# An audio tower on one core: a planner that counts overlapping neighbours, exponentials taken from the score banks, and later joins

## The chip, the cores and the metric

The kernel runs on one core of a Trainium2 chip. The metric is the device time of one execution in microseconds. Times below are the median of three runs, with their lowest and highest, or come from one profiled execution and its trace. Engines are named as in the profile: PE (TensorE matmul), PEld (its weight loads), DVE (VectorE), ACT (ScalarE), POOL (GpSimd), SP (the queue that issues DMAs).

## The reference

For each of 32 audio clips of 160000 samples:

```python
h = frames(x) @ DCT.T                          # 313 frames of 512 samples -> 512 features
a = layernorm(h)
Q, K, V = xpos(a @ W_Q), xpos(a @ W_K, downscale), a @ W_V       # 8 heads of 64
p = softmax(Q @ K.T) * Dmat                    # Dmat: per-head decay with distance
h = h + (silu(a @ W_G) * groupnorm(p @ V)) @ W_O
a = layernorm(h)
theta = a[..., None, :] / (1 + |W|) + B_param  # 256 units x 512 features, per frame
i = round(theta * 4096 / 2pi) mod 4096
s = sum(sin_table[i] * attn_sin, -1); c = sum(cos_table[i] * attn_cos, -1)
h = h + silu(c @ proj_cos.T + s @ proj_sin.T)
```

The costly part is the last layer: a sine and a cosine for each of 32 x 313 frames, 256 units and 512 features.

## The kernel before, in words

**Sines.** The 256 units are cut into 8 blocks of 32 (`UNITS`). A round (`ffn_round`, L746) treats one block for the sequences that are then in the ring, at most 8; a sequence joins at round `STARTS[q]`, stays 8 rounds (one for each block) and leaves. A round's work is cut into slots of 24 rows of 313 values (16 when the ring has one sequence). For each slot DVE computes integer indices from features and frequencies (L800, one operation for each unit, feature chunk and run of sequences, so a short ring means many short operations), adds a quarter turn (L816) and masks both copies (L823); ACT takes the sine of each copy (L837, two instructions of 12 x 2 x 313 = 7512 values); PE sums over features into four PSUM banks (L860). There are five index buffers and five sine buffers, and a slot needs two of each.

**Attention.** The front of the network (`attention`, L362) is done for one sequence at a time in one set of buffers and in the other four PSUM banks, and has to be finished before that sequence joins. Its stages: transform, layernorm, transpose, values (`rows` into `x.v`), then two halves of (two rotations, two sets of scores), exponentials, eight heads (transpose, decay, product), gate, group norm, output projection. A set of scores (L432) is, three times: a pair of matmuls into two banks, a maximum over each row on DVE (L448), and a subtraction that writes the scores minus the maximum to `x.prob` (L452). Later ACT takes exponentials in place from `x.prob`: two instructions of 3756 columns (L469) and sums on DVE (L484), or, in the *ACT mode*, 24 instructions of 313 columns which also sum (L473). The ACT mode, in which ACT also makes the copies out of PSUM, is chosen where the ring has at most `NARROW` sequences when the attention begins. Before the exponentials ACT loads their table, and after them it returns to the table with the sine (L477). Sequence 0 has an opening of its own (`opening`, L962); sequence 1 follows it at once.

**Order.** Nothing is scheduled by hand and nothing by the framework: `Plan` (L56) collects operations with a key (its due place), an engine, a duration in ns, and what they read and write. `emit` (L99) simulates the engines with these durations and issues the instructions in the order that comes out; on each engine the ready operation with the lowest key goes first. Results cross to another engine after 300 ns (`WAIT`), or 800 (`SLACK`) for the attentions. Each engine runs its instructions in that order. `lend` (L80): when ACT stands idle in the plan and DVE has more ready operations than the one it takes, ACT takes one of those for which a second version is given; index operations have one (L806).

**Due places.** A key counts slots of one sine: a sequence in a round is 2 x 32 x 4 / 24 = 10.67 keys. The attentions' starts are spread so that each is done `LEAD` keys before its sequence joins; the loop at L1297 takes the smallest spacing that some later sequence asks for, and each attention's steps get keys spread over its spacing (`SHARE`, L30).

Of the kernel before, what the change touches and what calls it, by code (L numbers as in the profile page):

```python
# [21 lines left out]
P = 128  # L22
# [33 lines left out]
class Plan:  # L56
# [13 lines left out]
    def add(self, key, eng, dur, fn, r=(), w=(), other=None):  # L70
# [9 lines left out]
    def lend(self, t, e, at, free, ready, coming):  # L80

        if ready["ACT"] or free["ACT"] > t or (coming["ACT"] and coming["ACT"][0][0] <= t):
            return None
        while coming["DVE"] and coming["DVE"][0][0] <= t:
            _, i = heapq.heappop(coming["DVE"])
            heapq.heappush(ready["DVE"], (self.ops[i][0], i))
        held = sorted(ready["DVE"])[int(free["DVE"] <= t):]
        for o in sorted((o for o in held if o[1] in self.other),
                        key=lambda o: (self.other[o[1]][0] > self.ops[o[1]][2], o)):
            if True:  # L90
                start = max(free["ACT"], at[o[1]])
                if coming["ACT"] and coming["ACT"][0][0] < start + self.OWN * self.other[o[1]][0]:
                    continue
                ready["DVE"].remove(o)
                heapq.heapify(ready["DVE"])
                return o[1], start
        return None

    def emit(self):  # L99
# [31 lines left out]
        left = len(ops)  # L131
        while left:
            best = None
            for e in free:
                if ready[e]:
                    t = free[e]
                elif coming[e]:
                    t = max(free[e], coming[e][0][0])
                else:
                    continue  # L140
                if best is None or t < best[0]:
                    best = (t, e)
            t, e = best
            lent = self.lend(t, e, at, free, ready, coming)
            if lent:
                i, t = lent
                e = "ACT"
                dur, fn = self.other[i]
            else:
# [15 lines left out]
        return max(free.values())  # L165
# [3 lines left out]
def tile_audio_tower(ctx: ExitStack, tc: tile.TileContext, t: dict, out: bass.AP):  # L169
# [192 lines left out]
    def attention(plan, keys, sq, x, eng, swap_m=None, early=False, quick=False):  # L362
# [13 lines left out]
        def residual(key, load):  # L376
            for i in range(NT):
# [20 lines left out]
        rows(plan, step("rows"), x, x.xnT, wv_d, (x.k("xnT"),), range(NT - 1, -1, -1),  # L398
             ("wv_d",))
        copy(plan, step("copy"), eng, NT * HOP, x.v[:N], W3.rearrange("n j (g d) -> n j g d", d=P),  # L400
             x.banks(0, 1, 2), hs)
        plan.add(step(), "POOL", 4000, lambda: nc.gpsimd.memset(x.v[0:1, : NT - 1], 0.0), (), hs)  # L402
# [4 lines left out]
        def rotary(g):  # L407
            key = step("rotary")
            y = x.sets[g % len(x.sets)]
            qk, kq = x.qk[g % 2], x.k("u", g % 2)  # L410
# [6 lines left out]
            else:  # L417
                copy(plan, key, eng, 2 * S, x.raw, y.W[:, 0:2, :S], y.banks(0, 1), probs[-1:])
                for i in range(2):
# [10 lines left out]
                     probs[-2:], (kq,))  # L430
# [27 lines left out]
        for half in range(2):  # L458
            for g in (2 * half, 2 * half + 1):
                rotary(g)  # L460
            for g in (2 * half, 2 * half + 1):
                scores(g)


        key = step("exps")
        for a0 in (0, H // 2):
            def exps(a0=a0):
                if eng == "DVE":
                    nc.scalar.activation(x.prob[:N, a0 : a0 + H // 2], x.prob[:N, a0 : a0 + H // 2],  # L469
                                         AF.Exp)  # L470
                for a in range(a0, a0 + H // 2):
                    for i in range(NT if eng == "ACT" else 0):
                        nc.scalar.activation(x.prob[:N, a, i, :], x.prob[:N, a, i, :], AF.Exp,  # L473
                                             accum_out=x.sm[:N, i, a : a + 1])
                if a0:

                    nc.scalar.activation(x.lu[:1, 0:1], x.lu[:1, 0:1], AF.Silu)  # L477
            plan.add(-1e9 if a0 else key, "ACT", 1400 + (7700 if eng == "ACT" else 3350), exps,
                     probs[a0 : a0 + H // 2] if early else probs if not a0 else (),
                     [*probs[a0 : a0 + H // 2], x.k("sm", a0), x.k("lu")])  # L480
        if eng == "DVE":
# [264 lines left out]
    def ffn_round(plan, k0, blk, ring, final):  # L746
# [25 lines left out]
        for parts in slots:  # L772
# [53 lines left out]
            for k in (1, 0):  # L826
# [11 lines left out]
                plan.add(key, "ACT", 115 + 0.8333 * E, sines, every(x[1 - k]),  # L838
# [617 lines left out]
```

## Time and profile before

| | |
|---|---|
| median of 3 runs | 18152.65 us (18149.81 to 18154.47) |
| the profiled execution | 18155.45 us |
| its span, first to last instruction | 18153.7 us |
| ACT busy | 17989.7 us, 99% |
| DVE busy | 17132.7 us, 94% |
| PE busy | 14314.5 us, 79% |
| granted TensorE clock | 0.935 |

Busy time is the union of an engine's instructions. A group line of the profile gives line, engine and operation, tiles and shapes, count, then busy us and mean ns of one, then the idle us just before them and what ended most of that. Neighbouring instructions of one engine can overlap by some 0.1 us, so a mean duration is longer than the distance between two starts. The answers by stretch give, for each stretch of the span, its length, the busy us of each engine (or of one line's instructions) with the count, the granted clock and the DMA share and rate.

### The profile page before, as it was taken

Reading aid. Unit: us, or ns where it says so; the run is one execution under the profiler, and the core shown is the slowest. Engines: PE = TensorE matmul, PEld = TensorE weight load, DVE = VectorE, ACT = ScalarE, POOL = GpSimd, SP = SyncE. Lnnn points to the kernel's source line nnn. Section 1 sums busy time; section 2 is a strip of 40 time slices with the busy share of each in tenths; the row PEclk is TensorE's granted clock in tenths of the full one; section 3 lists DMA queues with packets and bytes.
Section 4 is the critical chain, followed back from the end, with each engine's and each line's share of the span. In section 5 each row is a group of like instructions: output and inputs, shape, how many; then the busy total and the mean of one; then the engine's idle time right before and its main releaser. Section 6 shows DMA issues by size and latency. Waiting matters only on the chain.

```text
span 18153.7 us, 322090 instructions
## 1 busy us (share of the span) xinstructions
PE 14314.5 (79%) x146495; PEld 6447.3 (36%) x146495; DVE 17132.7 (94%) x12295; ACT 17989.7 (99%) x3448; POOL 126.5 (1%) x40
## 2 busy tenths in 40 slices
PE   8888888887778777878777787777777777766667
PEld 4434433433333333333333333333333333322222
DVE  8999999999999999999999999999999999888888
ACT  7999999999999999999999999999999999999999
POOL 0000000000000000000000000000000000000000
PEclk9999999999999999999999999999999999989889
DMA  3222211111111111111111111111111111100011
GB/s 115 74 63 64 67 56 57 53 51 47 45 52 53 53 52 41 53 54 51 51 50 47 53 53 53 52 41 53 54 51 50 48 48 54 46 28 27 28 33 58
DMA packets 603597, 943.16 MB, mean 52 GB/s; under 512 B 121290, under 2 KB 344138, under 8 KB 589430
## 3 DMA queue, kind: packets, MB, share of 16 engines
q1 hardware_dynamic: 602230, 922.56, 16.4%
q8 instruction: 1148, 18.81, 0.4%
q14 instruction: 219, 1.79, 0.0%
HBM read 818.35 MB, written 103.94 MB: 51 GB/s over the span
## 4 chain that ended last, share of the span: by engine, by line
ACT 40%; PE 18%; DVE 8%; issue 7%; DMA 0%; ACTq 0%; SPq 0%; DVEq 0%
ACT trig L837 40%; PE PS L860 15%; DVE ix L800 3%; DVE ix L823 2%; PE PS L341 2%; DVE ix L816 1%; PE PS L357 1%; ACT a_prob L469 0%; DMA a_u<-in_frames 0%; DVE part L882 0%; PE PS L561 0%; ACT L477 0%; DVE a_h L267 0%; PE PS L523 0%; ACTq L837 0%
## 5 line engine op out<-in xcount | busy, mean ns | idle before, releaser
L837 ACT ACTIVATE trig<-ix 128x7512 f32<-128x7512 int16 (+2 forms) x2780 | 17384.1, 6346 | 50.1 <-PE PS L860 30.6
L860 PE MATMUL PS<-trig,hot 128*32 128x313 f32 x131072 | 10449.9, 463 | 3662.4 <-ACT trig L837 3594.1
L860 PEld LDWEIGHTS PS<-trig,hot 128*32 128x32 f32 x131072 | 4391.7, 117 | 9590.2 <-ACT trig L837 4876.7
L800 DVE TENSOR_SCALAR ix<-xT,f 128x2504 int16<-128x2504 f32 (+7 forms) x5329 | 6418.7, 1264 | 90.4 <-ACT trig L837 67.1
L823 DVE TENSOR_SCALAR ix<-ix 128x7512 int16<-128x7512 int16 (+3 forms) x1668 | 5583.9, 3362 | 42.5
L816 DVE TENSOR_SCALAR ix<-ix 128x7512 int16<-128x7512 int16 (+2 forms) x1390 | 2908.8, 2093 | 553.3 <-ACT trig L837 450.7
L357 PE MATMUL PS<-a_xnT,a_ring 128*128 128x313 f32 x4960 | 1468.1, 439 | 8.9 <-DVE a_prob L425 6.9
L341 PE MATMUL PS<-a_ring,a_u 128*105 128x512 f32 x2232 | 1067.4, 611 | 53.6 <-DMA a_u<-in_frames 19.6
L357 PEld LDWEIGHTS PS<-a_xnT,a_ring 128*128 128x128 f32 x4960 | 893.4, 189 | 588.4 <-issue 276.5
L341 PEld LDWEIGHTS PS<-a_ring,a_u 128*105 128x105 f32 x2232 | 349.9, 171 | 629.3 <-issue 585.3
L341 PE MATMUL PS<-a_ring,a_xnT 128*105 128x512 f32 x744 | 353.9, 608 | 3.5 <-DVE a_xnT L267 1.8
L500 PE MATMUL PS<-ident,a_prob 105*105 105x105 f32 x2232 | 288.8, 272 | 70.5 <-DVE a_prob L512 47.1
L448 DVE TENSOR_REDUCE a_mx<-PS 105x2 f32<-105x626 f32 x372 | 298.6, 803 | 29.0 <-PE PS L443 28.9
L512 DVE TENSOR_TENSOR a_prob<-PS,a_u 105x939 f32<-105x939 f32 x248 | 280.3, 1130 | 38.4 <-PE PS L500 34.3
L500 PEld LDWEIGHTS PS<-ident,a_prob 105*105 105x105 f32 x2232 | 236.5, 176 | 223.7 <-issue 140.6
L452 DVE TENSOR_TENSOR a_prob<-PS,a_mx 105x626 f32<-105x626 f32 x372 | 301.3, 810 | 12.8
L443 PE MATMUL PS<-a_u 64*105 64x313 f32 x1488 | 258.9, 453 | 8.5 <-DVE a_prob L452 7.0
L523 PE MATMUL PS<-a_prob,a_h 105*64 105x313 f32 x1488 | 240.9, 443 | 6.6 <-DVE a_prob L512 6.5
L484 DVE TENSOR_REDUCE a_sm<-a_prob 105x6 f32<-105x1878 f32 x112 | 228.8, 2103 | 8.6 <-ACT a_prob L469 8.6
L402 POOL MEMSET a_h<- 1x1024 f32 x31 | 124.0, 4002 | 15023.3 <-DVE a_h L267 14393.9
L806 ACT ACTIVATE ix<-xT,f 128x313 int16<-128x313 f32 (+6 forms) x206 | 195.3, 1008 | 0.2
L425 DVE TENSOR_TENSOR a_prob<-PS,a_prob 128x1252 f32<-128x1252 f32 x124 | 180.7, 1457 | 10.5 <-PE PS L357 9.8
(157 smaller groups left out, 2606.0 us busy)
## 6 DMA issues: line engine op xcount, KB each, us to landing
hot<-in_hot SPq DMA_DIRECT2D x1344, 128.0 KB
xT<-xT_d SPq DMA_DIRECT2D x88, 1252.0 KB
a_u<-in_decay SPq DMA_DIRECT2D x248, 260.5 KB
a_ring<-in_proj SPq DMA_DIRECT2D x128, 256.0 KB
a_ring<-in_dct SPq DMA_DIRECT2D x124, 256.0 KB
a_ring<-wv_d SPq DMA_DIRECT2D x124, 256.0 KB
a_ring<-in_wq SPq DMA_DIRECT2D x124, 256.0 KB
a_ring<-in_wk SPq DMA_DIRECT2D x124, 256.0 KB
```

The source lines that it names most:

```text
L341: lambda c=c, i=i, k=k, to=to: nc.tensor.matmul(x.W[:N, to, :], lhsT[:, c, ROW0[i] : ROW0[i] + N], x.ring[k], start=(c == 0), stop=(c == N ...
L357: lambda c=c: nc.tensor.matmul(y.W[:, bank, :S], w[:, c, :], x.xnT[:, c, :], start=(c == 0), stop=(c == NC4 - 1)),
L443: nc.tensor.matmul(y.W[:N, b + a, :S], qk[a * DH : a * DH + DH, 0, ROW0[i] : ROW0[i] + N], qk[a * DH : a * DH + DH, 1, :], start=True, sto ...
L448: lambda b=b, m=m, y=y: nc.vector.tensor_reduce(m[:N], y.W[:N, b : b + 2, :S], AX.X, ALU.max),
L452: lambda i=i, b=b, m=m, y=y: nc.vector.tensor_tensor(x.prob[:N, 2 * g : 2 * g + 2, i, :], y.W[:N, b : b + 2, :S], m[:N].unsqueeze(2).to_br ...
L500: nc.tensor.transpose(y.W[:N, jj, ROW0[i] : ROW0[i] + N], x.prob[:N, a, i, ROW0[j] : ROW0[j] + N], ident[:N, :N],)
L512: nc.vector.tensor_tensor(x.prob[:N, a], y.W[:N, :NT, :S], w3, ALU.mult)
L800: nc.vector.tensor_scalar(ix[:, x[0], at * S : (at + nb) * S], xT[:, y, b0 * S : (b0 + nb) * S], f[:, 0, n : n + 1], f[:, 1, n : n + 1], A ...
L816: nc.vector.tensor_scalar(ix[:, x[1], :E], ix[:, x[0], :E], float(LUT // 4), None, ALU.add)
L823: nc.vector.tensor_scalar(ix[:, i, :E], ix[:, i, :E], LUT - 1, LUT // 2, ALU.bitwise_and, ALU.bitwise_xor)
L837: nc.scalar.activation(o, i, AF.Sin, bias=-PI32, scale=ANG)
L860: nc.tensor.matmul(sums_W[:, p, :][g * 32 : g * 32 + 32, :S], now["hot", hot[n // 4 * 4, c]][:, n % 4, k, :], trig[:, z, at * S : (at + 1) ...
```

## The change

The planner gets two constants: `OVER`, by which an engine is free again before an operation's end (85 ns on DVE, 100 on ACT, half the duration at most), and `AFTER`, 35 ns, which an operation waits for the result of one before it on its own engine. The duration of a sine grows from 115 to 197 ns plus 0.8333 ns a value. An operation may belong to a group; once ACT has begun one, ACT and DVE are *held*: in the plan, ACT issues only that group's operations, and DVE only these or operations of at most 900 ns, and nothing is lent, until ACT has done the last.

Sequences 1 to 7 (`burst`) do all four rotations first, with two of the query and key pairs kept in the buffer `x.h`, and then one group of 24 steps: a matmul into one bank, a maximum (negated) on DVE, and an exponential on ACT that reads that bank with the maximum as its bias, writes `x.prob` and sums. The subtraction, and the sums on DVE, are gone for them. The values, which use `x.h`, move behind the group. The starts, the lead, and the choice of the ACT mode change with it.

```diff
-STARTS = (0, 2, 4, *range(6, 35))
+STARTS = (0, 3, 5, 7, *range(10, 38))
-FROM, TO, LEAD, NARROW = -900.0, -899.0, 8.0, 2
+FROM, TO, LEAD, NARROW, BURSTS = -900.0, -899.0, 6.0, 1, 8
...
+    OVER = {"DVE": 85.0, "ACT": 100.0}
+    AFTER = 35.0
...
-        if ready["ACT"] or free["ACT"] > t or (coming["ACT"] and coming["ACT"][0][0] <= t):
+        if self.held or ready["ACT"] or free["ACT"] > t or (coming["ACT"] and coming["ACT"][0][0] <= t):
...
+    def next_held(self, e, at, free, ready, coming):
+
+        some = [(max(free[e], at[i]), self.ops[i][0], i) for _, i in (*ready[e], *coming[e])
+                if self.group.get(i) == self.held or (e == "DVE" and self.ops[i][2] <= self.SHORT)]
+        if not some:
+            return None
+        t = min(some)[0]
+        _, i = min((k, i) for s, k, i in some if s <= t)
+        return t, e, i
+
+    SHORT = 900.0
...
+                if self.held and e in ("ACT", "DVE"):
+                    t = self.next_held(e, at, free, ready, coming)
...
             fn()
+            if i in self.group and e == "ACT":
+                todo[self.group[i]] -= 1
+                self.held = self.group[i] if todo[self.group[i]] else None
             free[e] = t + dur
+            free[e] -= min(self.OVER.get(e, 0.0), dur / 2)
...
-                at[j] = max(at[j], end + (0.0 if same else self.wait[i]))
+                at[j] = max(at[j], end + (self.AFTER if same else self.wait[i]))
...
+        if not burst:
+            values()
+        if burst:
+            mine = x.h.rearrange("p i d -> p (i d)")[:, : NC4 * S].rearrange("p (g i s) -> p g i s", g=2, s=S)
+            qks, kqs = [*x.qk, mine[:, 0], mine[:, 1]], [*us, hs[0], hs[1]]
+        else:
+            qks, kqs = [*x.qk, *x.qk], [*us, *us]
...
+        def together():
+
+            gid = ("exps", sq)
+            n_all = 2 * NC4 * NT
+            for z in range(n_all):
+                g, i, a, b = z // 2 // NT, z // 2 % NT, z % 2, z % 4
+                qk = qks[g][a * DH : a * DH + DH]
+                m, km = x.mx[b // 2][:N, a : a + 1], x.k("mx", b)
+
+                def exps(hd=2 * g + a, i=i, b=b, m=m, z=z):
+                    nc.scalar.activation(x.prob[:N, hd, i, :], x.W[:N, b, :S], AF.Exp, bias=m, scale=1.0,
+                                         accum_out=x.sm[:N, i, hd : hd + 1])
+                    if z == n_all - 1:
+                        nc.scalar.activation(x.lu[:1, 0:1], x.lu[:1, 0:1], AF.Silu)
+                plan.slack = plan.WAIT
+                plan.add(-1e9 + z, "PE", 350, lambda i=i, b=b, qk=qk: nc.tensor.matmul(
+                    x.W[:N, b, :S], qk[:, 0, ROW0[i] : ROW0[i] + N], qk[:, 1, :], start=True, stop=True),
+                    (kqs[g], kqs[-1]), x.banks(b), group=gid)
+                plan.add(-1e9 + z, "DVE", 490, lambda b=b, m=m: nc.vector.tensor_reduce(
+                    m, x.W[:N, b, :S], AX.X, ALU.max, negate=True), x.banks(b), (km,), group=gid)
+                plan.add(-1e9 + z, "ACT", 510 + 1400 * (z in (0, n_all - 1)), exps, (km, *x.banks(b)),
+                         [probs[2 * g + a], x.k("sm", g // 2 * 4),
+                          *((x.k("lu"),) if z == n_all - 1 else ())], group=gid)
...
+        if burst:
+            for g in range(NC4):
+                rotary(g)
+            together()
+            step("scores"), step("scores"), step("scores"), step("scores"), step("exps")
+            values()
...
-        if eng == "DVE":
+        if eng == "DVE" and not burst:
...
-                plan.add(key, "ACT", 115 + 0.8333 * E, sines, every(x[1 - k]),
+                plan.add(key, "ACT", 197 + 0.8333 * E, sines, every(x[1 - k]),
...
-        narrow = len(rings[int(np.searchsorted(key_of, k, "right")) - 1]) <= NARROW
-        events.append((k, 1, lambda k=k, e=e, i=i, narrow=narrow: attention(
-            plan, lambda x: k + (e - k) * x, 2 + i, A, "ACT" if narrow else "DVE",
-            quick=QUICK[0] <= i + 2 < QUICK[1])))
+        r = len(rings[int(np.searchsorted(key_of, k, "right")) - 1])
+        events.append((k, 1, lambda k=k, e=e, i=i, r=r: attention(
+            plan, lambda x: k + (e - k) * x, 2 + i, A, "ACT" if r <= NARROW and i < 16 else "DVE",
+            quick=QUICK[0] <= i + 2 < QUICK[1], burst=i + 2 < BURSTS)))
```

More of the change, by code (lines that the diff above doesn't have):

```diff
@@ L131, in emit @@
         left = len(ops)
+        self.held, todo = None, {}
+        for i, g in self.group.items():
+            todo[g] = todo.get(g, 0) + (ops[i][1] == "ACT")
         while left:
@@ L164, in emit @@
                     heapq.heappush(coming[ops[j][1]], (at[j], j))
-        return max(free.values())
+        return max(self.OVER.get(e, 0.0) + v for e, v in free.items())
 @with_exitstack
@@ L360, in columns, with attention @@
             )
-    def attention(plan, keys, sq, x, eng, swap_m=None, early=False, quick=False):
+    def attention(plan, keys, sq, x, eng, swap_m=None, early=False, quick=False, burst=True):
         done = [0.0]
@@ L395, in attention, with values @@
         copy(plan, step("copy"), eng, NC4 * S, x.xnT, x.W[:, :, :S], x.banks(0, 1, 2, 3), (x.k("xnT"),))
[L398 to L402, printed above, removed]
+        def values():
+            rows(plan, step("rows"), x, x.xnT, wv_d, (x.k("xnT"),), range(NT - 1, -1, -1),
+                 ("wv_d",))
+            copy(plan, step("copy"), eng, NT * HOP, x.v[:N], W3.rearrange("n j (g d) -> n j g d", d=P),
+                 x.banks(0, 1, 2), hs)
+            plan.add(step(), "POOL", 4000, lambda: nc.gpsimd.memset(x.v[0:1, : NT - 1], 0.0), (), hs)
+        if not burst:
[5 more added lines that the diff above has]
+            qks, kqs = [*x.qk, *x.qk], [*us, *us]
         plan.add(step(), "SP", DMA_NS, lambda: nc.sync.dma_start(x.table, t["turn_qk"]),
@@ L429, in rotary @@
                          qk, x.turn[:, 0:2], x.turn[:, 2:4], ALU.add),
[L430 removed]
+                     probs[-2:], (kq, *(hs if burst and g == 2 else ())))
         def scores(g):
```

61 lines of the change are left out of this document (38 added, 23 removed).

## The prediction

> **What bounds the kernel now.** I read the busy shares and the 40 slices first. ScalarE (ACT) is busy for 99% of the span, and only the first slice shows a 7. In the waits of ACT, nothing but the opening is over 20 us. ACT is the path, so the time is the sum of what stands on ACT plus its idle time.
>
> ```profile
> PE 14314.5 (79%) x146495; PEld 6447.3 (36%) x146495; DVE 17132.7 (94%) x12295; ACT 17989.7 (99%) x3448; POOL 126.5 (1%) x40
> ...
> L837 ACT ACTIVATE trig<-ix 128x7512 f32<-128x7512 int16 (+2 forms) x2780 | 17384.1, 6346 | 50.1 <-PE PS L860 30.6
> ...
> L806 ACT ACTIVATE ix<-xT,f 128x313 int16<-128x313 f32 (+6 forms) x206 | 195.3, 1008 | 0.2
> ```
>
> (A group line reads: busy us, mean ns of one | idle before it.) The sines are 17384 us and cannot shrink. What can shrink is small: 195 us of L806, which are index operations lent from VectorE (DVE) to ACT, and ACT's idle time, 164 us in all. Then I asked, stage by stage, where L806 stands (first block) and how busy the engines are there (second block). Columns of the first: stretch, its length, ACT busy (count).
>
> ```profile
> 0.00:300.00 300.00, 34.45 (x61) 0.97 0.41 125
> 300.00:700.00 400.00, 36.50 (x46) 0.92 0.30 89
> 700.00:1200.00 500.00, 26.08 (x22) 0.96 0.22 65
> 1200.00:2400.00 1200.00, 54.40 (x43) 0.95 0.20 62
> 2400.00:4000.00 1600.00, 22.17 (x15) 0.95 0.18 56
> 4000.00:16000.00 12000.00, 12.31 (x5) 0.93 0.16 50
> ```
>
> ```profile
> 300.00:700.00 400.00, 345.53 (x3070) 162.00 (x3063) 385.43 (x488) 397.40 (x164) 5.67 (x2) 0.92 0.30 89
> 700.00:1200.00 500.00, 450.71 (x3938) 213.09 (x3933) 468.50 (x459) 483.06 (x148) 4.74 (x1) 0.96 0.22 65
> 1200.00:2400.00 1200.00, 1005.15 (x9708) 484.60 (x9707) 1157.46 (x967) 1193.46 (x244) 9.72 (x3) 0.95 0.20 62
> 2400.00:4000.00 1600.00, 1339.64 (x13221) 621.63 (x13220) 1552.97 (x1170) 1594.80 (x283) 10.16 (x3) 0.95 0.18 56
> 4000.00:16000.00 12000.00, 9414.71 (x98682) 4209.65 (x98680) 11436.90 (x7333) 11985.07 (x2014) 93.20 (x22) 0.93 0.16 50
> ```
>
> (PE, weight loads, DVE, ACT, POOL.) Nine tenths of the lending lies before 4000 us, while the rings are short. From 300 to 4000 ACT idles 31 us and DVE 136 us; in the same stretch DVE never waits for an index buffer (L816), though it does so for 175 us between 4000 and 14000. So **before 4000 us DVE is the engine that is late, and ACT pays**; afterwards ACT has all it needs. Of the opening's 105 idle us before 300, I expect nothing to change: the waits there are for sequence 0's own chain.
>
> **The room on DVE.** One sequence in one round (a sequence-round, 1/256 of the sines) takes ACT 17385/256 = 67.9 us. DVE's share depends on the ring: 128/r index operations, whose starts lie 351, 515, 678, 842, 1005, 1168, 1330 and 1493 ns apart for r = 1 to 8, and 5.33 times 2.04 + 3.99 us of L816 and L823, 32.2 us. So the room left per sequence-round is -10, 2.7, 6.8, 8.8, 10, 10.8, 11.4, 11.8 us. One attention needs about 80 us of DVE: between 4000 and 16000, ACT has 11732 us of sines = 172.8 sequence-rounds; 172.8 x 56.1 = 9694 of DVE's 11437 us, the other 1743 belong to 21.6 attentions. While ACT does an attention's own work (9.3 us for the exponentials, 2.4 for both Silus) DVE gains that too, so 68 us net. In the ACT mode of sequences 1 to 3, 41.
>
> **Check on before.** Sequences 2 to 6 are spaced 53.9 keys apart (sequence 6 joins after 26 sequence-rounds: (26 x 10.67 - 8)/5), that is 5.05 sequence-rounds, then 6. Need less room is 52, 11, 27, 18, 18, 4 and 2 us, and about 40 of sequence 1: 172. With DVE's 136 idle us, 308 must come from ACT. A lent operation moves its DVE time (351 ns for 540 on ACT, so 0.65) and also gives DVE the time it takes: 1.65 for 1. Up to 4000 us, 187 lent operations, net of 0.1 us overlap each, took 155 us: 155 x 1.65 + 31 idle = 287. The account closes within 7%, and I use it for the change.
>
> **Part 1, the held visit (sequences 1 to 7).** It removes 12 subtractions (L452) for each sequence, and for 4 to 7 four sums (L484); 12 reductions become 24 half as wide; exponentials become 24 small ones that read the score banks.
>
> ```profile
> L452 DVE TENSOR_TENSOR a_prob<-PS,a_mx 105x626 f32<-105x626 f32 x372 | 301.3, 810 | 12.8
> L448 DVE TENSOR_REDUCE a_mx<-PS 105x2 f32<-105x626 f32 x372 | 298.6, 803 | 29.0 <-PE PS L443 28.9
> ...
> L484 DVE TENSOR_REDUCE a_sm<-a_prob 105x6 f32<-105x1878 f32 x112 | 228.8, 2103 | 8.6 <-ACT a_prob L469 8.6
> ...
> L469 ACT ACTIVATE a_prob<-a_prob 105x3756 f32<-105x3756 f32 x56 | 183.7, 3327 | 0.3
> ...
> L1175 ACT ACTIVATE ix<-PS,trig 105x313 f32<-105x313 f32 x24 | 12.2, 520 | 15.0 <-DVE trig L1170 15.0
> ```
>
> DVE, net of 85 ns overlap: 12 x 0.72 + 12 x 0.72 + 4 x 2.02 = 25.4 us become 24 x 0.395 = 9.5 (a 313-wide copy from the banks takes 480): 15.9 us less for 4 to 7, 7.8 for 1 to 3, 87 in all. In the held visit DVE may run only short operations (900 ns planned), which wastes some 4 us each: 59 net.
>
> ACT: today a visit takes 2 loads of 1.29 us, and 2 x 3.24 us, 9.3 with the tail; in the ACT mode of 1 to 3, 24 of 313 columns (L473) with starts 447 ns apart, 13.6. The new exponential is the opening's L1175: its starts, with the accumulator read, lie 497 ns apart. Lower bound 24 x 0.497 + 2.9 = 14.8. It is a chain over four banks, though: matmul 0.43, reduction 0.48, exponential 0.6 and the hops between, some 2 us for four, so 0.5, if PE and DVE answer at once. If DVE slips one three-wide index operation (0.68) before each reduction it is 1.07, a visit of 28.6. I take 0.55, near the row that does the same thing: 16.1 us. Seven visits: 113 for 78 today, **+35 us on ACT** (26 to 122). A matmul of PE queued between the scores (L860, PE is 90% busy here) holds the same chain and is in that range. The values are moved behind the visit: 4 loads of SP's queue behind the 8 of the rotations, 12 matmuls of 0.6 us, a copy of 1.75 and POOL's memset of 4.0. They now stand, 13 us, between the last exponential and the first product of a head. That lies beside index work of DVE while an attention has its 390 us of spacing; without that cover it would be 13 us for each of 7, and no more DVE work.
>
> The trace splits the same exponentials at 497 ns against 277 (3327/12) for one head's rows in the long form. [...]
>
> **Part 2, later joins.** I counted the lists of the program: 45 rounds for 42, 1393 slots for 1390 (6 more sines, 0.6 us of fixed time), 5887 index operations for 5535: 352 x 0.197 us = 69 us more DVE. Sequences 1 to 10 join after 3, 7, 13, 23, 27, 31, 36, 41, 47, 53 sequence-rounds instead of 2, 6, 12, 16, 21, 26, 32, 38, 45, 52; from 11 on nothing differs. Spacing is now (41 x 10.67 - 6)/7 = 61.6 keys, 5.78 sequence-rounds. Need less room, with the visits of part 1 (33 net for sequence 2, 48 for 3 to 7): 54, 14, 1, 8, 0, 0, 7, 3, and 33 of sequence 1: **120 instead of 172**. Sequence 3 leaves the ACT mode: its copies, -6 us on ACT, are in this.
>
> **Part 3, the planner.** Neighbours do overlap: index starts 842 ns apart last 928, sines 6355 apart last 6450. The old plan charged DVE 85 ns too much on each operation, and so lent more than was needed; of DVE's 136 idle us, 60 are waits for PE by an operation placed too early or late. I take those away: 76 left (bounds 40, if the small gaps shrink too, to 136, if nothing does).
>
> [...]
>
> **The sum.** Need 120 + 76 = 196; less 31 idle, 165/1.65 = 100 lent; 131 with the idle, for 186 today: -55 (with 136 instead of 76: -19; with 40: -77). The five lent operations between 4000 and 16000 go too, since DVE waits for ACT there: -12. So -67 + 35 - 6 + 1 = **-37 us**. The profiled execution took 18155.4 (2 us more than its span), so 18118; the median of the runs is 2.8 lower: **18115**. A measurement here can tell about 0.2%, 36 us, from no change, and the forecast sits on that edge.
>
> **Rivals.**
> 1. *Lending all but ends* (0.25): the plan's 85 ns were most of the lending, need falls to DVE's floor and half of the 100 goes: 18065. For: DVE's 136 idle us beside 155 lent. Against: L816 never waited there.
> 2. *Nothing net* (0.17): 69 us of new index work eats the 59 from the visits, DVE stays as late as it was (-19 instead of -55) and ACT keeps the visits' price: 18152. Also the case that the chip doesn't keep the order the plan holds.
> 3. *Slower* (0.18): the visit itself. PE's sine matmuls and short index operations get in between, 1.07 us per exponential: +122 instead of +35, 18203. It decides from 0.78 us (21.5 us a visit), where the gain is gone; over 0.2% slower from 0.99. For: PE is 90% busy. Against: DVE and PE have little short work left once ACT has stopped making sines.
> 4. *The forecast* (0.40): between 18085 and 18140.
>
> Faster by over 0.2%: rival 1 and 0.23 of the forecast's 0.40, 0.48. Within: the rest of it and rival 2, 0.34; slower: rival 3, 0.18. The range reaches rivals 1 and 3: 18040 to 18210.
>
> **What would show it.** L806 falls from 206 to some 110, with ACT idle between 300 and 4000 still about 30; visits of L1175's kind about 0.55 us apart, 16 us; L452 at 288 and L484 at 96; index operations 352 more. I am wrong if visits run over 21 us, if ACT idles instead of lending, or if DVE's idle time stays.

## The result and the profile after

The changed kernel takes **18235.3 us** (median of 5 runs, 18232.81 to 18238.14) against 18152.65 us: a ratio of 1.0046, 95% interval 1.0031 to 1.006. It is slower by 83 us. The profiled execution took 18232.88 us, its span is 18231.1 us, the granted clock 0.940.

The page of the changed kernel, first the busy shares and then the groups whose lines answer to L837, L452 and L484 of before; L914 is now the sine, L937 PE's sum over features, and L893 DVE's quarter turn (before, L816).

```profile
PE 14712.8 (81%) x146495; PEld 6260.7 (34%) x146495; DVE 17047.2 (94%) x12739; ACT 17973.8 (99%) x3585; POOL 132.5 (1%) x40
...
L914 ACT ACTIVATE trig<-ix 128x7512 f32<-128x7512 int16 (+2 forms) x2786 | 17383.6, 6328 | 117.0 <-PE PS L937 91.8
...
L893 DVE TENSOR_SCALAR ix<-ix 128x7512 int16<-128x7512 int16 (+2 forms) x1393 | 2901.8, 2083 | 729.3 <-ACT trig L914 688.3
...
L497 DVE TENSOR_TENSOR a_prob<-PS,a_mx 105x626 f32<-105x626 f32 x288 | 231.7, 806 | 0.0
...
L561 DVE TENSOR_REDUCE a_sm<-a_prob 105x6 f32<-105x1878 f32 x96 | 201.8, 2103 | 1.0 <-ACT a_prob L546 1.0
```

ACT is less busy than before, by 16 us, and the span is 77 us longer. So ACT waits more, and 92 of its idle us now stand ahead of a sine that waits for PE to hand back a buffer (31 before). DVE, which had been the late engine, now waits 688 us in L893 for ACT to hand back index buffers (451 in L816 before).

The lent index operations (L883, L806 before) by stretch: length, ACT busy (count), clock, DMA share, GB/s.

```profile
0.00:300.00 300.00, 25.62 (x45) 0.94 0.39 118
300.00:1200.00 900.00, 28.07 (x40) 0.97 0.27 79
1200.00:2400.00 1200.00, 7.48 (x6) 0.97 0.23 67
2400.00:4000.00 1600.00, 14.40 (x8) 0.96 0.20 58
4000.00:6000.00 2000.00, 2.47 (x1) 0.94 0.17 50
6000.00:16000.00 10000.00, 0.00 (x0) 0.94 0.17 50
```

There are 111 of them in the whole span, where there were 206. The groups of ACT by form show the second thing that is new, the table loads of the exponentials:

```profile
L546 ACT ACTIVATE a_prob<-a_prob 105x3756 f32<-105x3756 f32 x48 | 160.2, 3337 | 0.5
L513 ACT ACTIVATE a_prob<-PS,a_mx 105x313 f32<-105x313 f32 x168 | 85.3, 526 | 19.6 <-DVE a_mx L521 19.0
L546 ACT ACT_TABLE_LOAD x48 | 61.6, 1283 | 0.9
...
L914 ACT ACT_TABLE_LOAD x24 | 30.8, 1283 | 0.4
L554 ACT ACT_TABLE_LOAD x24 | 30.8, 1283 | 0.4
```

The 48 long exponentials of sequences 8 to 31 have 48 loads ahead of them, and 24 sines and 24 Silus have one each: four loads for each sequence, where two would do. ACT's timeline in one such place (start, us, engine, line):

```profile
4322.21 1.28 ACT L546 ACT_TABLE_LOAD   x1
4323.51 3.34 ACT L546 ACTIVATE a_prob<-a_prob 105x3756 f32<-105x3756 f32 x1
4326.86 1.28 ACT L914 ACT_TABLE_LOAD   x1
4328.16 6.46 ACT L914 ACTIVATE trig<-ix 128x7512 f32<-128x7512 int16 x1
4334.64 1.28 ACT L546 ACT_TABLE_LOAD   x1
4335.93 3.34 ACT L546 ACTIVATE a_prob<-a_prob 105x3756 f32<-105x3756 f32 x1
```

A sine stands between the two halves of one sequence's exponentials, with the table changed for it and changed back.

Every microsecond of ACT's span can be put down to one kind of instruction, or to idle time, if each instruction is counted from its own start, or from the end of the one before it where that is later, to its own end. This account is worked out from both traces and ends with ACT's last instruction; its differences add up to the span's difference of 77 us:

| us of ACT's span | before | after | difference |
|---|---|---|---|
| sines | 17368.5 | 17372.8 | +4 |
| lent index operations | 186.9 | 82.0 | -105 |
| idle | 159.6 | 252.8 | +93 |
| exponentials, accumulator reads | 216.3 | 248.2 | +32 |
| table loads (66, then 112) | 84.7 | 143.7 | +59 |
| copies and others | 133.3 | 127.1 | -6 |

ACT's idle time by stretch, from the same account (before, after): to 300 us 104.6 and 113.1; to 1200, 19.5 and 28.5; to 2400, 6.5 and 22.0; to 4000, 5.2 and 29.3; to 6000, 1.6 and 21.8; to 16000, 13.3 and 19.2; to the end 8.8 and 19.0. Its growth doesn't lie where the lending went away: up to 2400 us lending fell by 87 us and idle time grew by 33; from 2400 to 6000 lending fell by 5 and idle time grew by 44.

### The profile page after: what moved, and what is told of

It reads as the page before. It is cut to its first block, busy times and chain, and to the rows that moved or that the text cites. A ratio compares the mean times of both kernels' runs of the same rounds, so it can differ in the third digit from the quotient of the medians.

```text
span 18231.1 us, 322825 instructions
## 1 busy us (share of the span) xinstructions
PE 14712.8 (81%) x146495; PEld 6260.7 (34%) x146495; DVE 17047.2 (94%) x12739; ACT 17973.8 (99%) x3585; POOL 132.5 (1%) x40
## 5 line engine op out<-in xcount | busy, mean ns | idle before, releaser
L914 ACT ACTIVATE trig<-ix 128x7512 f32<-128x7512 int16 (+2 forms) x2786 | 17383.6, 6328 | 117.0 <-PE PS L937 91.8
L937 PE MATMUL PS<-trig,hot 128*32 128x313 f32 x131072 | 10651.6, 460 | 3240.3 <-ACT trig L914 3184.9
L937 PEld LDWEIGHTS PS<-trig,hot 128*32 128x32 f32 x131072 | 4255.3, 116 | 9401.9 <-ACT trig L914 4426.0
L877 DVE TENSOR_SCALAR ix<-xT,f 128x2504 int16<-128x2504 f32 (+7 forms) x5776 | 6596.8, 1195 | 160.6 <-ACT trig L914 113.4
L900 DVE TENSOR_SCALAR ix<-ix 128x7512 int16<-128x7512 int16 (+4 forms) x1672 | 5580.4, 3352 | 25.9
L893 DVE TENSOR_SCALAR ix<-ix 128x7512 int16<-128x7512 int16 (+2 forms) x1393 | 2901.8, 2083 | 729.3 <-ACT trig L914 688.3
L393 PE MATMUL PS<-a_xnT,a_ring 128*128 128x313 f32 x4960 | 1600.8, 451 | 23.3 <-DMA a_ring<-in_wq_s 6.1
L377 PE MATMUL PS<-a_ring,a_u 128*105 128x512 f32 x2232 | 1117.0, 618 | 16.9 <-issue 7.1
L600 PE MATMUL PS<-a_prob,a_h 105*64 105x313 f32 x1488 | 302.1, 466 | 6.0 <-DVE a_prob L589 5.9
L497 DVE TENSOR_TENSOR a_prob<-PS,a_mx 105x626 f32<-105x626 f32 x288 | 231.7, 806 | 0.0
L493 DVE TENSOR_REDUCE a_mx<-PS 105x2 f32<-105x626 f32 x288 | 225.3, 804 | 0.0
L561 DVE TENSOR_REDUCE a_sm<-a_prob 105x6 f32<-105x1878 f32 x96 | 201.8, 2103 | 1.0 <-ACT a_prob L546 1.0
L377 PEld LDWEIGHTS PS<-a_ring,a_xnT 128*105 128x105 f32 x744 | 109.0, 171 | 207.6 <-issue 174.5
```

The source lines that it names most:

```text
L377: lambda c=c, i=i, k=k, to=to: nc.tensor.matmul(x.W[:N, to, :], lhsT[:, c, ROW0[i] : ROW0[i] + N], x.ring[k], start=(c == 0), stop=(c == N ...
L393: lambda c=c: nc.tensor.matmul(y.W[:, bank, :S], w[:, c, :], x.xnT[:, c, :], start=(c == 0), stop=(c == NC4 - 1)),
L493: lambda b=b, m=m, y=y: nc.vector.tensor_reduce(m[:N], y.W[:N, b : b + 2, :S], AX.X, ALU.max),
L497: lambda i=i, b=b, m=m, y=y: nc.vector.tensor_tensor(x.prob[:N, 2 * g : 2 * g + 2, i, :], y.W[:N, b : b + 2, :S], m[:N].unsqueeze(2).to_br ...
L600: nc.tensor.matmul(y3.W[b * DH : (b + 1) * DH, 3, :S], x.v[:N, jj, g, b * DH : (b + 1) * DH], x.prob[:N, 2 * g + b, jj, :], start=(jj == 0 ...
L877: nc.vector.tensor_scalar(ix[:, x[0], at * S : (at + nb) * S], xT[:, y, b0 * S : (b0 + nb) * S], f[:, 0, n : n + 1], f[:, 1, n : n + 1], A ...
```

## The experiments

Medians are given with the ratio to the kernel before, run beside it on the same chip (about 18151 us). The theory after the result had two parts: the new planner splits exponentials, which costs some 60 us, and the end of the lending has come back as idle time. Fourteen kernels were run to tell the parts apart. Below, "planner" is `OVER`, `AFTER` and the new sine duration, "joins" the new `STARTS`, `LEAD` and `NARROW`, "visits" the held visits. Edits are to the changed kernel where nothing else is said; unchanged lines between the edits are left out.

### The exponentials put back together

```diff
-            for a0 in (0, H // 2):
-                def exps(a0=a0):
+            def exps():
+                for a0 in (0, H // 2):
...
-                plan.add(-1e9 if a0 else key, "ACT", 1400 + (7700 if eng == "ACT" else 3350), exps,
...
+            plan.add(key, "ACT", 2800 + 2 * (7700 if eng == "ACT" else 3350), exps,
+                     (), [*probs, x.k("sm", 0), x.k("sm", 4), x.k("lu")])
```

> The changed kernel with one edit: for sequences 8 to 31 both halves of the exponentials are one operation of the planner, so no sine can be put between them. Theory: the changed planner frees ACT 100 ns before an operation's end but lets its successor on ACT start 35 ns after that end, so the second half is never ready in time, a sine goes first, and the table of Exp and that of the sine are loaded once more for each of 24 sequences, 48 loads of 1.28 us. Table loads then fall from 112 to 64 and the time by about 60 us, to 18175. Rival: the extra loads stand beside waits for PE that ACT would have anyway; then loads fall as well, but ACT's idle time (253 us) grows by most of 60 and the time stays above 18215.

Measured: **18171.27 us**, 1.0012 (1.0003 to 1.0021): 64 us less than the changed kernel. In the groups of ACT by form of this kernel, L547 is the long exponential, L553 the Silu behind it:

```profile
L547 ACT ACTIVATE a_prob<-a_prob 105x3756 f32<-105x3756 f32 x48 | 157.4, 3327 | 0.3
...
L547 ACT ACT_TABLE_LOAD x24 | 30.8, 1283 | 0.4
L553 ACT ACT_TABLE_LOAD x24 | 30.8, 1283 | 0.4
```

The count of loads goes from 112 to 64, 48 x 1.29 = 62 us, and with it the time. Idle (253.8 us) and lending (83.9) hardly move. The split is one cause, and it is the larger part of the 83 us; the rest of the change, taken together, is 20 us slower than before.

How the split comes about can be read in the code with the timeline. The second half depends on the first, by the buffer that both write, so it becomes ready 35 ns after the first half's *end* (`AFTER`). ACT, though, is free 100 ns before that end (`OVER`). In these 135 ns only others are ready, and the planner gives ACT to a sine; the second half's key of -1e9 no longer helps.

### Each part alone

The planner alone, then the joins alone, then the visits alone:

```diff
# the planner alone
-STARTS = (0, 3, 5, 7, *range(10, 38))
+STARTS = (0, 2, 4, *range(6, 35))
-FROM, TO, LEAD, NARROW, BURSTS = -900.0, -899.0, 6.0, 1, 8
+FROM, TO, LEAD, NARROW, BURSTS = -900.0, -899.0, 8.0, 2, 0
-    attention(plan, lambda x: FROM + (TO - FROM) * x, 1, A, "ACT", None, True)
+    attention(plan, lambda x: FROM + (TO - FROM) * x, 1, A, "ACT", None, True, burst=False)
# the joins alone
-FROM, TO, LEAD, NARROW, BURSTS = -900.0, -899.0, 6.0, 1, 8
+FROM, TO, LEAD, NARROW, BURSTS = -900.0, -899.0, 6.0, 1, 0
-    OVER = {"DVE": 85.0, "ACT": 100.0}
-    AFTER = 35.0
+    OVER = {"DVE": 0.0, "ACT": 0.0}
+    AFTER = 0.0
-                plan.add(key, "ACT", 197 + 0.8333 * E, sines, every(x[1 - k]),
+                plan.add(key, "ACT", 115 + 0.8333 * E, sines, every(x[1 - k]),
-    attention(plan, lambda x: FROM + (TO - FROM) * x, 1, A, "ACT", None, True)
+    attention(plan, lambda x: FROM + (TO - FROM) * x, 1, A, "ACT", None, True, burst=False)
# the visits alone: old STARTS, LEAD 8, NARROW 2, BURSTS 8, and OVER, AFTER and the sine as in the joins alone
```

> The kernel before with the planner's part alone (overlap, the 35 ns, the longer sine); starts, lead, ACT mode and exponentials as before. Theory: the split exponentials cost 28 x 2.57 = 72 us, less lending saves about 70 us, and waits of ACT for PE stay near the 31 us of before: 18155. Rival: the waits for PE that the changed kernel shows (92 us for 31) come from the planner's new order; then 18215. Second rival: no split without the visits; then 18085.

Measured: 18375.62 us, 1.0123 (1.011 to 1.0137), above theory and rivals alike. 126 loads, 77 us more than before, are the split again; idle time is 345 us where before has 160, and 110 of it lies from 300 to 1200 us (20 before). Lending fell by 53 us. ACT's timeline from 330 us:

```profile
331.06 4.38 ACT L914 ACTIVATE trig<-ix 128x5008 f32<-128x5008 int16 x1 [2.09 <-PE PS L937]
351.45 1.20 ACT L301 COPY a_u<-PS 128x1252 f32<-128x1252 f32 x1 [16.01 <-PE PS L364]
361.93 9.71 ACT L883 ACTIVATE ix<-xT,f 128x626 int16<-128x626 f32 x12 [9.28 <-DMA xT<-xT_d]
382.55 6.46 ACT L914 ACTIVATE trig<-ix 128x7512 f32<-128x7512 int16 x1 [10.90 <-DVE ix L900]
```

ACT waits, 16.0, 9.3 and 10.9 us, for a sequence that is about to join and whose attention isn't done: with the early starts of before, the new planner's attention comes too late.

> The kernel before with the later joins alone (starts, lead, ACT mode for rings of one); old planner, old exponentials. Theory by the account of rooms: need less room is 62, 34, 21, 28, 17, 13, 7, 3 and 40 of sequence 1, 225 instead of 172, so 33 us more lending: 18185, with lending up from 206 to some 240 operations. Rival: the later joins are what brings ACT's waits for PE (more rounds with a ring of three, where PE's groups of 32 columns are three instead of four); then these waits rise from 31 to about 90 us and the time is 18240. Second rival: the looser due places save lending; then 18110.

Measured: 18311.03 us, 1.0088 (1.0074 to 1.0102): **160 us slower**, again above theory and rivals. Lent operations take 272 us, and 70 us of the idle time lie between 6000 and 16000 us, where before has 13.

> The kernel before with the held visits of sequences 1 to 7 alone; old planner, old starts. Theory: visits cost 32 us on ACT, DVE is relieved and lending falls by about 50 us: 18133, with lending down to some 150 operations. Rival: what is held starves the engines round it (PE's sine sums and DVE's long operations come late after a visit), ACT's waits rise by some 50 us and the time is 18190.

Measured: **18141.1 us**, 0.9994 (0.9986 to 1.0003), the lowest of all the kernels, though not to be told from before. Exponentials cost 28 us more, lent operations fall by 39, idle grows by 9: here lending went away and idle time hardly came for it.

### The parts in pairs

Joins with visits (the changed kernel with `OVER` and `AFTER` at 0 and the old sine), and planner with visits (the changed kernel with the old `STARTS`, `LEAD` 8, `NARROW` 2, and the exponentials in one operation):

> The changed kernel with the old planner: later joins and held visits, no overlap, no 35 ns, sines of 115 ns plus 0.8333 a value; the old planner splits no exponentials. Theory, by adding single steps (joins alone +160, visits alone -10, and need of DVE in the account 52 us less): about 18260, with lent time near 200 us. Rival: later joins and visits belong together and bring the time under that of before, 18130; then the planner's part is what made the changed kernel slower.

> The kernel before with the new planner and the held visits, the exponentials of sequences 8 to 31 in one visit, old starts, lead and ACT mode. Theory: with the old starts the new planner misses the early due places (ACT stood 110 us idle between 300 and 1200 us in the kernel with the planner alone, beside the copy of a sequence that was to join), and the later joins are what mends that: 18376 less 77 for the split, less 30 for the visits, 18270, with idle time between 300 and 1200 over 60 us. Rival: the split was all that was wrong with the planner: below 18171, and the joins cost time.

Measured: joins with visits 18292.35 us, 1.0077 (1.0062 to 1.0092), with 69 us of idle time from 6000 to 16000, 32 above the theory; planner with visits 18223.34 us, 1.004 (1.0025 to 1.0054), with 63 us of idle time from 300 to 1200, between theory and rival.

**The parts don't add up.** The joins cost 160 us with the old planner (151 beside the visits: 18292 less 18141), and they *gain* 52 with the new planner and the visits (18171 less 18223). The later joins are the price of the new planner, and repay it only there.

### The lead by itself

In the trace of the joins alone, the extra idle time from 6000 on comes every 560 us, once in each full round. The timeline of such a place, PE's weight loads and the DMA queue left out:

```profile
6304.94 4.07 DVE L900 TENSOR_SCALAR ix<-ix 128x15024 int16<-128x15024 int16 x1
...
6308.93 0.48 DVE L959 COPY part<-PS 128x313 f32<-128x313 f32 x1
6309.32 1.75 DVE L303 COPY a_h<-PS 105x1536 f32<-105x1536 f32 x1
...
6314.19 0.39 ACT L962 COPY part<-PS 128x313 f32<-128x313 f32 x1
...
6314.34 8.08 PE L937 MATMUL PS<-trig,hot 128*32 128x313 f32 x84 [8.12 <-ACT trig L914]
...
6320.18 6.47 ACT L914 ACTIVATE trig<-ix 128x7512 f32<-128x7512 int16 x1 [3.22 <-PE PS L937]
```

At a round's end the sums must be copied out of PSUM, by four copies (L959 on DVE, L962 on ACT), before PE may begin the next round's in the same banks. Here a mask of 4.07 us (L900) goes ahead of the third copy, and a copy of an attention (L303) behind it. The last copy goes behind a sine on ACT and begins 16.7 us after the first; PE starts 8.1 us late, and ACT then waits 3.2 us for a sine buffer. (PE's wait is put down to the sine; whether it needed that or a copy, the trace doesn't settle.) With full rings there is one attention for one round, so what `LEAD` decides, the attention's place in the round, is the same in all of them. The theory: `LEAD` 6 alone sets this collision. Its test is the kernel before with `LEAD` 6 and nothing else, and the joins alone with `LEAD` 8:

```diff
# kernel before
-FROM, TO, LEAD, NARROW = -900.0, -899.0, 8.0, 2
+FROM, TO, LEAD, NARROW = -900.0, -899.0, 6.0, 2
# the joins alone
-FROM, TO, LEAD, NARROW, BURSTS = -900.0, -899.0, 6.0, 1, 0
+FROM, TO, LEAD, NARROW, BURSTS = -900.0, -899.0, 8.0, 1, 0
```

> The kernel before with one number changed: a lead of 6 keys instead of 8. Theory: the lead alone brings the meeting of copies in each full round: ACT idle between 6000 and 16000 us up from 13 to some 70 us, lent time up from 12 to 40, time about 18245. Rival: the lead does nothing by itself; 18150 within 25 us.

> The kernel with the later joins alone (18311), but with the lead of before, 8 keys instead of 6. Theory: at full rings one attention takes one round, so it stands in every round at the same place, set by the lead; with 6 keys its first copy out of PSUM meets the copies of the round's sums on DVE, one of these goes to ACT behind a sine, PE waits 8 us and ACT 3 us, 18 rounds long. With 8 keys ACT's idle time between 6000 and 16000 us falls from 70 to under 25 us and the lent time there from 41 to some 12; the time is about 18225, and the rest of the loss, some 70 us, is the short rings. Rival: the place in the round comes from the order of the whole plan and not from the lead; then idle and lent time there stay over 80 us together, and the time within 30 us of 18311.

Measured: 18259.29 us, 1.006 (1.0043 to 1.0076), **107 us from one constant**; and 18213.59 us, 1.0034 (1.0021 to 1.0047), 97 us less than with 6. In the kernel before with `LEAD` 6, the lent operations and the engines (PE, weight loads, DVE, ACT, POOL) from 6000 to 16000 us, and ACT's waits there (us, times, longest):

```profile
6000.00:16000.00 10000.00, 44.44 (x18) 0.93 0.17 50
```

```profile
6000.00:16000.00 10000.00, 7778.09 (x81539) 3476.93 (x81538) 9422.00 (x6042) 9935.08 (x1690) 54.13 (x18) 0.93 0.17 50
```

```profile
ACT trig L837 <- PE PS L860: 62.4, 23, 5.2
```

The same three in the kernel before:

```profile
6000.00:16000.00 10000.00, 12.31 (x5) 0.93 0.16 50
```

```profile
6000.00:16000.00 10000.00, 7842.16 (x82174) 3501.21 (x82170) 9514.87 (x6101) 9986.72 (x1678) 72.22 (x18) 0.93 0.16 50
```

```profile
ACT trig L837 <- PE PS L860: 11.0, 6, 5.5
```

52 us less ACT work and 32 us more lending among it: 84 of the 107 us lie in the full rounds, 18 of them (one POOL memset for each attention), 4.7 us a round. That is shown. What collides is the mask, though, and not the attention's copy, as the expectation above has it. In all 18 full rounds with `LEAD` 6, of this kernel and of the joins alone, the mask stands ahead of the third copy, and ACT waits 2.8 us or more each time. In the kernel before it does so only in the last of the 18, where no such copy of an attention stands near, and there too ACT waits 5.5 us. In the other 17, the attention's copy (L267) comes 0.4 to 1.9 us after the first of the round's, quarter turn and mask come later, the third copy goes ahead of the mask, and ACT waits 1.5 us in all. In the changed kernel the mask stands ahead in the last round alone, no operation is lent from 6000 to 16000, and 19 us are idle. What the joins cost beyond it with the old planner, 62 us, is mostly lending: 245 us against 187.

### Where the new planner's idle time comes from

Three theories: DVE's overlap of 85 ns makes the plan too tight; the slack of 800 ns for an attention's results is too small; `AFTER` lets others overtake an operation whose input comes from its own engine, so an attention's chains are torn. The first two are edits on the kernel with the exponentials put together:

```diff
-    OVER = {"DVE": 85.0, "ACT": 100.0}
+    OVER = {"DVE": 0.0, "ACT": 100.0}
# another kernel
-SLACK, PATIENT, QUICK = 800.0, 18000, (2, 32)
+SLACK, PATIENT, QUICK = 1600.0, 18000, (2, 32)
```

> The changed kernel with the exponentials of sequences 8 to 31 in one visit (18171) and, in the planner, no overlap on DVE (85 to 0); ACT's overlap and the 35 ns stay. Theory: the planner's quicker DVE is what trades lending for idling (lent time 187 to 84 us, idle 160 to 254 us); so lent time goes up to some 140 us, ACT's idle time down to some 200, and the total stays within 20 us of 18171. Rival: the idle time comes from ACT's own new numbers or from the joins; then the idle time stays near 254 while lending rises, and the time is 18230.

> The changed kernel with the exponentials in one visit and, in the planner, 1600 ns instead of 800 before another engine may use a result of an attention. Theory: PE stands in order behind attention matmuls whose operands come later than planned, so it hands sine buffers back late and ACT waits (92 us for 31 before); with more room these waits halve and the time is about 18135. Rival: the waits are not from that margin, ACT's waits for PE stay near 90 us, and a longer chain of an attention costs lending: 18171 to 18190.

Measured: without DVE's overlap 18326.96 us, 1.0095 (1.008 to 1.011), lent 211, idle 270; with the larger slack 18326.61 us, 1.0098 (1.0083 to 1.0113), lent 148, idle 355. Neither margin brings the idle time down in total, and each costs some 155 us. Outside 6000 to 16000 us, though, the first does what its theory says, only at too high a price: 27 us less idle for 106 more lent.

The third: an operation is ready as soon as its own engine is free, so that its key decides. It is tried on the changed kernel, on the planner alone, and on planner and visits:

```diff
-                at[j] = max(at[j], end + (self.AFTER if same else self.wait[i]))
+                at[j] = max(at[j], free[e] if same else end + self.wait[i])
```

> The changed kernel with one line of the planner changed: an operation that needs a result of its own engine is ready when that engine is free, not 35 ns after the end. Theory: with the 35 ns, and the engine free 85 or 100 ns before the end, no dependent operation is ever ready in time, so another one overtakes it at every step of an attention (of 124 turns of the rotations, 124 were followed at once by their sum before, none in the changed kernel); that splits the exponentials, and it makes each attention longer and its PE work ragged, so ACT waits. Then table loads are 64, ACT's idle time falls from 253 to about 190 us, and the time is 18130. Rival: overtaking splits the exponentials and does no more harm; then the time is that of the kernel with one visit, 18171, and the idle time 250.

> The kernel before with the planner's part alone, as in the run of 18376, but without overtaking (the same line). Theory: sequences 1 and 2 finish in time again (the last step of sequence 2's group norm stood at 561 us before and at 679 with the planner alone), the idle time between 300 and 1200 us falls from 110 to some 30, table loads from 126 to 66, and the time is 18160 or less. Rival: the planner's quicker DVE itself makes it too hopeful with the old due places: 18260, with idle time between 300 and 1200 us over 70.

> Old starts, lead and ACT mode, with the held visits and the planner without overtaking. Theory: visits and planner both save lending and nothing is late: 18223 of the same with overtaking and one visit, less some 90: 18130, under the kernel before. Rival: the later joins are needed for the planner in any form: 18200 or more, and the changed kernel with the same line is faster than this one by 50 us.

Measured: changed kernel 18286.49 us, 1.0074 (1.0062 to 1.0087), idle 349; planner alone 18316.98 us, 1.0092 (1.0076 to 1.0107), idle 395; planner and visits 18279.2 us, 1.0072 (1.0059 to 1.0084), idle 342. The edit does what it should: loads are down to 64 and 66, and the rotation's sum again follows its product at once on DVE, in 106 and 120 of 124 places for the first two, where the changed kernel has none. Idle time rises all the same, so the forecasts fell. That overtaking splits the exponentials is shown. What it does besides can be read at the end of a full round. From the changed kernel with this edit:

```profile
9084.28 4.07 DVE L900 TENSOR_SCALAR ix<-ix 128x15024 int16<-128x15024 int16 x1
9088.26 0.48 DVE L959 COPY part<-PS 128x313 f32<-128x313 f32 x1
9088.66 1.75 DVE L303 COPY a_h<-PS 105x1536 f32<-105x1536 f32 x1
...
9099.24 6.47 ACT L914 ACTIVATE trig<-ix 128x7512 f32<-128x7512 int16 x1 [5.63 <-PE PS L937]
```

The same place in the changed kernel with the exponentials put together (18171), where the lines are L898, L957 and L912:

```profile
9025.08 1.75 DVE L303 COPY a_h<-PS 105x1536 f32<-105x1536 f32 x1
9026.74 0.47 DVE L957 COPY part<-PS 128x313 f32<-128x313 f32 x1
9027.14 4.06 DVE L898 TENSOR_SCALAR ix<-ix 128x15024 int16<-128x15024 int16 x1
...
9036.17 6.47 ACT L912 ACTIVATE trig<-ix 128x7512 f32<-128x7512 int16 x1 [1.64 <-PE PS L935]
```

The mask needs the quarter turn that ran just before it on DVE. With overtaking, another operation (here L303, of the attention) takes the place between the two, and the third copy goes ahead of the mask. Without it the mask follows at once and the copies come late. So it is in all 18 full rounds of the three kernels, and 87 to 92 us of the idle time of each stand there; in 18171 and in the planner with visits (18223) it is so in the last round alone. Idle and lent time from 6000 to 16000 come to 99 us in the first kernel, for 18 in 18171: 81 of the 115 us by which it is slower. In the third they come to 107, for 36 in 18223: 71, though it is only 56 slower, so the rest of its span gained. Here, then, overtaking helps. Whether another `LEAD` would keep the mask back without it, as in the kernel before, was not tried.

The last takes `AFTER` from PE alone, with the exponentials put together:

```diff
-                at[j] = max(at[j], end + (self.AFTER if same else self.wait[i]))
+                at[j] = max(at[j], end + ((self.AFTER if e != "PE" else 0.0) if same else self.wait[i]))
```

> The changed kernel with the exponentials in one visit (18171), and the 35 ns left out for PE alone, so that PE's chains of four matmuls into one bank stand together again while DVE's dependent operations are still overtaken. Theory: most of ACT's waits for PE (92 us) come from sine sums that break these chains; they fall to some 50 and the time is 18130. Rival: it is DVE's overtaking that counts: no change, 18165 to 18175.

Measured: 18226.5 us, 1.0042 (1.0028 to 1.0056), 55 us slower than with it, where the theory was 18130 and the rival no change. PE's projections stand in 597 unbroken runs again (584 before, 1062 in the changed kernel), idle is 261 us and lent 143. This doesn't show that torn chains on PE are better. L303 comes later in the round here, the mask is ahead of the third copy in 14 of 18 full rounds, and idle and lent time from 6000 to 16000 are 89 us for 18, more than the whole 55; outside that stretch idle time is 23 us lower and lending 18 higher. Without DVE's overlap, and with the larger slack, the mask is ahead in 13 and in all 18 rounds, and this stretch holds 65 and 42 of the 155 us.

## Why the prediction was wrong

The forecast was 18115; 18235 lies outside its range, and the sign is wrong. Step by step:

- **Part 3 lacked a step.** I priced the overlap as room gained on DVE, and didn't ask what a planner does whose engine is free *before* the result of its last operation is. It splits table-sharing neighbours: 46 loads more in all, 59 us by the account, 64 by the run that joins the halves. The sum had this term at nothing. It makes the loss clear: without it the kernel is 20 us slower than before, with it 83.
- **The lending term: the amount was right, its worth was not.** "165/1.65 = 100 lent" came out as 82 us, with 111 operations for some 110. But "131 with the idle, for 186" failed. Lending fell by 105 us and idle time rose by 93, so the two come to -12 where I had -67 (to -31 without the 19 us that belong to the visits, below). I had listed "if ACT idles instead of lending" as what would make me wrong. Of the 93, 61 stand ahead of sines that wait for PE: 30.6 us before, a row that "nothing but the opening is over 20 us" passed over, 91.8 after. Part 3 also took DVE's idle time between 300 and 4000 us from 136 down to 76. It stayed at 129, of which 45 are now waits of index work (L877, L893) for ACT. That idle time took the place of lending is not shown: the two changed in different stretches, and the visits alone lost 39 us of lending for 9 of idle time. It came with the new planner: the planner alone has 186 us more of it than the kernel before. What makes PE late there is **open**; the edits on DVE's margin, the slack, overtaking and PE's chains don't decide it, since each moved the mask ahead of the copies as well.
- **The visits were right in kind, a little low in size.** Predicted 16.1 us each and 0.55 us for an exponential; measured, from the first exponential's start to the last's end, 14.0 to 16.6 us, median steps 503 to 513 ns with a few up to 2.9 us, and two loads of 1.29: some 17.8 us. By the same 78 us for before that is +47 for +35; the account has 32 us of work and 19 of waits. L521, the reduction of half the width, takes 479 ns for the 480 assumed. The rival of 1.07 us didn't happen: the slower result that it stood for came true by another mechanism.
- **The lead was taken as harmless.** I treated it through the spacing of the first sequences alone. With the old planner it is worth about 100 us, in the full rounds, where I expected no change. In the changed kernel this doesn't show, since there the mask stays behind the third copy in 17 of 18 rounds. That the oversight cost nothing here was luck.
- **Counts and small terms held**: L497 and L561 have 288 and 96 as foreseen, copies and others -6 for -6, sines +4 for +1, index operations 5887. The opening's idle time rose from 105 to 113 us, where I expected no change.

Together: -31 for lending and idle time, +51 for the visits with their waits, +59 for the loads, +4 for the sines and -6 for the rest are the 77 us of the span. The lending that the change removed was real, but ACT's idle time grew by nearly as much, and the split and the visits' price came on top. The best version found keeps the visits alone, 18141 us, and it cannot be told from the kernel before.

## What to carry to other kernels

In a planner that counts overlap, the time at which an engine is free and the time at which its own results count as ready must fit together, or anything that has to stay together (here, instructions of one activation table: 48 loads more, 64 us) must be one operation. Where an engine takes on lent work, count its lent and its idle time together: less of the one is a gain only if the other stays. A periodic order multiplies a collision by its rounds (here 4.7 us by 18), so a constant that shifts the phase is to be tried by itself, and a test that changes the order is to be looked at for such a collision before its total is read; parts of a change to a scheduler are to be tried in pairs too, since one can repay the other.

## What the runs showed of the hardware

- The 112 loads of an activation table in the changed kernel took ACT 1283 ns each. Each but the first, which has no instruction ahead of it, began 4 to 19 ns behind the instruction before it, and the next one began 11 or 12 ns behind the load: in the timeline above, the load at 4322.21 is followed by the exponential at 4323.51, 1.30 us later, and the exponential that ends at 4326.85 by the next load at 4326.86.
- In the seven visits, an exponential of 313 columns straight from PSUM, with its accumulator read, took median steps of 503 to 513 ns in a chain over four banks in which PE and DVE both stand in every link, though DVE's maximum (mean 479 ns) is nearly as long as the step. At 18 places ACT did wait for the maximum, 19.0 us in all.
- Neighbours on DVE overlapped in the records: in the timeline of the joins alone, the copy at 6308.93 lasts 0.48 us and the next instruction starts at 6309.32, 0.39 us later.
